# One-hot tables of a token's slot: two wide operations or one operation for each column, with the pieces of work around them moved

## The chip, the cores and the metric

The kernel runs on one core of a Trainium2 chip. A core has five engines, each with a queue of its own that it works through in order: TensorE (PE, matrix products, with PEld for the loading of its weights), VectorE (DVE), ScalarE (ACT), GpSimd (POOL) and SyncE (SP, which here only issues transfers). Engines wait for each other by semaphores. The metric is the time of one execution on the device in microseconds (us); lower is better. The kernel before takes 642.78 us, the median of three runs (641.9 to 643.16).

## What is computed

A layer normalisation of x (2 x 2048 tokens of 256 channels) feeds two branches, and both are added to x. One is a recurrent attention (RWKV), the other a mixture of eight experts of which each token uses two:

```python
k = (x * time_mix_k + last_x * (1.0 - time_mix_k)) @ Wk.T      # v, r in the same way
wkv = _wkv_scan(jnp.exp(k), v, td)      # den = den * td + kt ; num = num * td + kt * vt
out = jax.nn.sigmoid(r) * wkv @ Wo.T
...
scores = jax.nn.relu(jnp.einsum('bsd,de->bse', x, Wr) + br)
_, topk_idx = jax.lax.top_k(scores, K)
...
h = jax.nn.relu(jnp.einsum('bsd,edh->ebsh', x, W1) + b1[:, None, None, :])
y = jnp.einsum('ebsh,ehd->ebsd', h, W2) + b2[:, None, None, :]
out = jnp.einsum('bse,ebsd->bsd', router_weight, y)
```

The kernel does not compute all experts for all tokens. It sorts the tokens by expert and computes, for each expert, the tokens that chose it.

## The kernel before

The 4096 tokens are handled as 32 groups of 128 (NT = 32), and for the attention as 8 blocks of 512 tokens (NB = 8). There are four stretches of work.

**Front (0 to about 60 us).** The blocks are normalised, transposed and scored for the router. `table` in DRAM receives the normalised rows for later gathering.

**Routing (about 60 to 106 us).** Each of the 4096 x 2 choices gets a slot. There are NU = 74 units of 128 slots each. First the counts: two products (L650) give `pre`, whose half 1 (with `ones`) is the count of each expert in each group and whose half 0 (with `upper`) is the rank within the group. The scan L664 sums half 1. Some fifty tiny operations on VectorE follow, and at L773 to L778 each choice has its slot, cut into `lo` (its place in the unit, 0 to 127) and `hi` (its unit, 0 to 73). Then the map is inverted: for each slot, which token? This is a product of one-hot tables. For each of the 64 columns (2 choices x 32 groups) a table of `lo` (128 x 128) is the weights, and a table of `hi` times the token's number (128 x 74) is the moving operand; the 64 products are summed in `inv` (L873). VectorE builds the tables in eight chunks of CH = 8 columns: `oh_a` from `lo`, `oh_b` from `hi` (both by comparison with a ramp, L854), and `oh_t` = `oh_b` x `token` (L865). The tables are f16 with columns laid in pairs, so that each of the three operations covers the whole chunk at once. From `inv` come `into` (the row that a slot's result goes to) and `frm` (the row that it is gathered from), L879 to L886. `experts_of_places` (L790) finds which expert owns each unit; one product, `whose`, spreads it over the partitions, and `whose_i` holds it as an integer. SP reads `whose_i` and loads that expert's weights.

**Experts (about 113 to 607 us).** 32 steps of two or three units. A step gathers its tokens from `table` (POOL, L987, by `frm`), scales them (`unnorm`, L997), transposes them (`xp`, L1021), multiplies by the expert's `w1` (`hp`, L1032) and `w2` (`yp`, L1045), and adds the result to DRAM. The first step can start when `whose_i` has let SP load its weights and `frm` has let POOL gather its rows. VectorE does the attention's scans between.

**End (607 to 642 us).** The attention's last product (`op`, L1125) is added to what the experts left in DRAM and stored, block by block.

The order on every engine is written out by hand: the program's order is each queue's order. Two generators are used to fill gaps. `mix(n)` (L416) emits n blends of the attention's inputs on VectorE: two operations of 128 x 512 each, from a part that ScalarE has prepared ahead (`preparer`, L383). `some(n)` (L448) emits n pieces of the attention's projections on TensorE: four products of 128 x 512 (named `p`, L437), with ScalarE's eviction behind them. A block takes six pieces: two with `wk`, two with `wv`, two with `wr`, and each pair needs its own mix. In the table loop, `MIX` and `SOME` (L848) say after which chunk's tables a mix is put, and after which chunk's products a piece. The pieces are thus TensorE's work while VectorE builds tables, and there is a mix to be made for every two pieces. Blocks 5, 6 and 7 are mixed and projected around the tables; the last four pieces stand around L1067 to L1070, ahead of and behind `turn(0)`, which transposes the first step's tokens.

Of the kernel before, what the change touches and what calls it, by code (L numbers as in the profile page):

```python
# [26 lines left out]
def rwkv_moe_block(  # L27
# [21 lines left out]
    nc = tc.nc  # L49
    P = 128  # L50
    B, T, C = x.shape
    E, _, H = w1.shape
    K = 2
# [5 lines left out]
    NB = NTOK // TB  # L59
    BPS = T // TB  # L60
    NT = NTOK // P
# [13 lines left out]
    NU = U0 + 2 * NPAIR + NRARE  # L75
# [38 lines left out]
    rout = routing.enter_context(tc.tile_pool(name="rout", bufs=1))  # L114
# [76 lines left out]
    )  # L191
    CH = 8

    def ramp(nm, n):
        t = rout.tile([P, n, 2], F16, name=nm)
        nc.gpsimd.iota(
            t, [[1, n], [0, 2]], base=0, channel_multiplier=0,
            allow_small_or_imprecise_dtypes=True,
        )
        return t  # L200

    lo_iota, hi_iota = ramp("lo_iota", P), ramp("hi_iota", NU)
    at_pair = rout.tile([P, 1], F32, name="at_pair")
    at_unit = place[:, 1:2]
    wlim = rout.tile([P, 2 * E], F32, name="wlim")
# [11 lines left out]
    ones = const.tile([P, P], BF16, name="ones")  # L217
# [198 lines left out]
    def mix(n):  # L416
        for _ in range(n):
            next(blending)
# [29 lines left out]
    def some(n):  # L448
        for _ in range(n):
            next(projected)  # L450


    def rt(nm, shape=(P, NT, E), dtype=F32, tag=None):
        return rout.tile(list(shape), dtype, tag=tag or nm, name=nm)
# [59 lines left out]
    def vec(i, c):  # L514
# [14 lines left out]
    upper = const.tile([P, P], BF16, name="upper")  # L529
# [3 lines left out]
        pattern=[[1, P]], channel_multiplier=-1,  # L533
    )

    token = rout.tile([P, NT], F16, name="token")
    for i in range(2):
        nc.gpsimd.iota(
            token[:, i * HT : (i + 1) * HT], [[P, HT]], base=(-NTOK // 2, 1)[i],
            channel_multiplier=1, allow_small_or_imprecise_dtypes=True,  # L540
# [4 lines left out]
    for n, size in ((NTRI, 3), (NPAIR, 2), (NRARE, 1)):  # L545
# [3 lines left out]
            base=NTOK, channel_multiplier=1, allow_small_or_imprecise_dtypes=True,  # L549
# [96 lines left out]

    pre = ps_t.tile([P, 2, E * NT], F32, tag="pt", name="pre")
    hot_e = hot.rearrange("p t e -> p e t")
    for i, m in enumerate((upper, ones)):
        nc.tensor.matmul(  # L650
            pre[:, i, :].rearrange("p (e t) -> p e t", e=E), m, hot_e, start=True, stop=True
        )
# [121 lines left out]
    half = rt("half", (P, 2, K * NT), I32)  # L774
    nc.vector.tensor_scalar(half[:, 0, :], posi, P - 1, None, ALU.bitwise_and)
    nc.vector.tensor_scalar(half[:, 1, :], posi, 7, None, ALU.logical_shift_right)
    lohi = rt("lohi", (P, 2, K * NT), F16)
    nc.vector.tensor_copy(lohi, half)  # L778
    lo, hi = lohi[:, 0, :], lohi[:, 1, :]
    mix(0)  # L780
    some(2)


    whose_i = const.tile([P, NW], I32, name="whose_i")
# [3 lines left out]
    whose = ps_t.tile([P, NW], F32, tag="pt", name="whose")  # L788

    def experts_of_places():  # L790

        nc.vector.tensor_scalar(
            at_pair, place[:, 0:1], 0.5, NPAIR / 2, ALU.mult, ALU.add
        )
        nc.vector.tensor_copy(offs[:, 1:2], full)
        nc.vector.tensor_tensor(at_pair, at_pair, place[:, 0:1], ALU.min)
        lim = rt("lim", (P, 2, E))
        nc.vector.tensor_tensor(
            lim, fcum[:, 0:2, :], offs.unsqueeze(2).to_broadcast([P, 2, E]), ALU.add
        )  # L800
# [12 lines left out]
        nc.vector.tensor_scalar(  # L813
            held[:, 2, 0:E], fcum[:, 3, :], place[:, 0:1], None, ALU.is_le
        )
        by = rt("by", (P, 3))
        nc.vector.tensor_reduce(by, held, AX.X, ALU.add)
        paired = rt("paired", (P, 1))
        nc.vector.tensor_scalar(paired, nth, 0.0, None, ALU.is_lt)
        expert = rt("expert", (P, 1))  # L820
        nc.vector.tensor_scalar(
            expert, by[:, 0:1], by[:, 1:2], paired, ALU.subtract, ALU.mult
        )
        nc.vector.tensor_scalar(expert, expert, by[:, 1:2], float(E - 1), ALU.add, ALU.min)
        on_row = rt("on_row", (P, NW), BF16)
        nc.vector.tensor_scalar(
            on_row[:, W3:NW], ident[:, 0:NTRI], by[:, 2:3], float(E - 1), ALU.mult, ALU.min
        )
        nc.vector.tensor_scalar(on_row[:, 0:W3], ident[:, 0:W3], expert, None, ALU.mult)
        nc.tensor.matmul(whose, ones, on_row, start=True, stop=True)  # L830
        nc.vector.tensor_copy(whose_i, whose)

    def experts_later():
        last = rt("last", (P, 2))
# [10 lines left out]

    inv = ps_y.tile([P, NU], F32, tag="py", name="inv")
    opool = routing.enter_context(tc.tile_pool(name="opool", bufs=3))
    MIX, SOME = (0, 1, 0, 1, 0, 1, 0, 1), (1, 1, 1, 1, 1, 1, 1, 1)  # L848
    for i0 in range(0, K * NT, CH):

        tables = []
        for nm, n, src, ramp2 in (("a", P, lo, lo_iota), ("b", NU, hi, hi_iota)):
            t = opool.tile([P, CH // 2, n, 2], F16, tag=f"oh_{nm}", name=f"oh_{nm}_{i0}")
            nc.vector.tensor_tensor(  # L854
                t,
                ramp2.unsqueeze(1).to_broadcast([P, CH // 2, n, 2]),
                src[:, i0 : i0 + CH].rearrange("p (a b) -> p a b", b=2).unsqueeze(2)
                .to_broadcast([P, CH // 2, n, 2]),
                ALU.is_equal,
            )  # L860
            tables.append(t)
        a, bq = tables
        bt_ = opool.tile([P, CH // 2, NU, 2], F16, tag="oh_t", name=f"oh_t_{i0}")
        t0 = i0 % NT
        nc.vector.tensor_tensor(  # L865
            bt_, bq,
            token[:, t0 : t0 + CH].rearrange("p (a b) -> p a b", b=2).unsqueeze(2)
            .to_broadcast([P, CH // 2, NU, 2]),
            ALU.mult,
        )  # L870
        mix(MIX[i0 // CH])
        for i in range(CH):
            nc.tensor.matmul(  # L873
                inv, a[:, i // 2, :, i % 2], bt_[:, i // 2, :, i % 2],
                start=(i0 + i == 0), stop=(i0 + i == K * NT - 1),
            )
        some(SOME[i0 // CH])
    empty = rt("empty", (P, NU))
    nc.vector.scalar_tensor_tensor(empty, inv, 0.0, less, ALU.is_equal, ALU.mult)  # L879
    row = rt("row", (P, NU))  # L880
# [3 lines left out]
    nc.vector.scalar_tensor_tensor(into, row, float(NTOK // 2), empty, ALU.add, ALU.add)  # L884
    frm = const.tile([P, NU], I32, name="frm")
    nc.vector.tensor_scalar_min(frm, into, float(NTOK - 1))  # L886
    mix(1)
    some(2)
    experts_of_places()
    some(1)  # L890
    mix(1)
    some(2)
    mix(1)
    experts_later()
    routing.close()
# [68 lines left out]
    def load_first(s):  # L964
        ev = expert_of(s)
        pool = wpool if s % 3 else w1_own
        b1_sb = pool.tile([P, NH], F32, tag="b1", name=f"b1_{s}")
        nc.sync.dma_start(b1_sb, b1cols[bass.ds(ev, 1)].rearrange("a p h -> p (a h)"))
        w1_sb = pool.tile([P, NC, H], F32, tag="w1", name=f"w1_{s}")
        nc.sync.dma_start(w1_sb, w1[bass.ds(ev, 1)].rearrange("a (c p) h -> p (a c) h", p=P))  # L970
        weights[s, 1] = (w1_sb, b1_sb)
# [22 lines left out]
    def unnorm(s):  # L994

        for g in rows_of[s]:
            nc.vector.tensor_scalar(  # L997
                g[:, 0:C], g[:, 0:C], g[:, C + 3 : C + 4], None, ALU.mult
            )
# [64 lines left out]
    load_first(0)  # L1064
    load_second(0)
    load_first(1)
    some(1)  # L1067
    unnorm(0)
    turn(0)
    some(2)  # L1070
    gate(0)
    unnorm(1)
    gate(1)
# [4 lines left out]
    for s in range(NSTEP):  # L1078
# [8 lines left out]
        b, o = divmod(s, NC)  # L1087
# [26 lines left out]
    def as_rows(b, i):  # L1114
        return kvr[b][:, i].rearrange("p c t -> p (c t)").rearrange("p (n d) -> p n d", d=C)
# [4 lines left out]
    for i, (b, t) in enumerate(late):  # L1120
        pool, tag = pools[i // 2 % 4]
        op = pool.tile([P, 2, C], F32, tag=tag, name=f"op_{b}_{t}")
        for k in range(2):
            for c in range(NC):
                nc.tensor.matmul(  # L1125
                    op[:, k, :], kvr[b][:, 0, c, ts(t + k, P)], wo_sb[:, c, :],
                    start=(c == 0), stop=(c == NC - 1),
                )
        done = as_rows(b, 1)[:, t : t + 2, :]
        nc.vector.tensor_tensor(done, op, done, ALU.add)  # L1130
        if b == NB - 1:
            (nc.scalar, nc.sync)[i % 2].dma_start(out_l[b, :, t : t + 2, :], done)
        elif t:
            nc.scalar.dma_start(out_l[b], as_rows(b, 1))
# [61 lines left out]
```

## Time and profile before

One execution was profiled. Its own time was 643.74 us, of which the span of the instructions is 642.0.

| what | us |
|---|---|
| median of three runs | 642.78 |
| the profiled execution | 643.74 |
| its span | 642.0 |
| `hp` of the first step starts | 113.11 |
| the attention's last product starts | 607.68 |

Busy time by stretches of 20 us (a row is a stretch; the columns are the engines' busy us):

| stretch | PE | DVE | ACT | POOL | mean DMA GB/s |
|---|---|---|---|---|---|
| 60 to 80 | 19.99 | 16.82 | 13.38 | 0.88 | 162 |
| 80 to 100 | 18.30 | 19.54 | 10.75 | 0.71 | 0 |
| 100 to 120 | 20.00 | 12.65 | 8.82 | 10.17 | 254 |
| 120 to 140 | 20.00 | 13.26 | 6.34 | 6.32 | 228 |

The table stage is the row from 80 to 100. The clock granted to TensorE was full (1.00) in all four. Two instructions that overlap on one engine are counted once. In the timelines that follow, a line with xN stands for N like instructions in a row, from the first's start to the last's end; an instruction may start before the record of the one ahead of it on the engine ends, so the cost of one in a run is best read from start to start. A time in brackets is how long the engine stood idle before the row, and for whom.

### The profile page before, as it was taken

Reading aid. Unit: us, or ns where it says so; the run is one execution under the profiler, and the core shown is the slowest. Engines: PE = TensorE matmul, PEld = TensorE weight load, DVE = VectorE, ACT = ScalarE, POOL = GpSimd, SP = SyncE. Lnnn points to the kernel's source line nnn. Section 1 sums busy time; section 2 is a strip of 40 time slices with the busy share of each in tenths; the row PEclk is TensorE's granted clock in tenths of the full one; section 3 lists DMA queues with packets and bytes.
Section 4 is the critical chain, followed back from the end, with each engine's and each line's share of the span. In section 5 each row is a group of like instructions: output and inputs, shape, how many; then the busy total and the mean of one; then the engine's idle time right before and its main releaser. Section 6 shows DMA issues by size and latency. Waiting matters only on the chain.

```text
span 642.0 us, 8628 instructions
## 1 busy us (share of the span) xinstructions
PE 629.6 (98%) x2870; PEld 480.0 (75%) x2870; DVE 356.0 (55%) x814; ACT 207.7 (32%) x402; POOL 230.4 (36%) x201
## 2 busy tenths in 40 slices
PE   8999999999999999999999999999999999999995
PEld 3554444878687877878888888888888888888884
DVE  7996897767677684866888852222222222222132
ACT  5786654332322221322233332222222222222200
POOL 5780006035353352424344136334344433322200
PEclk9999999999999999999999999999999999999999
DMA  7835505857546364656556998765666666653177
GB/s 238 264 118 169 100 0 138 291 173 189 173 108 203 92 207 125 176 169 181 173 176 184 354 264 272 216 178 173 180 181 191 211 204 213 200 157 92 24 259 276
DMA packets 83944, 117.04 MB, mean 182 GB/s; under 512 B 14796, under 2 KB 70168, under 8 KB 83768
## 3 DMA queue, kind: packets, MB, share of 16 engines
q1 hardware_dynamic: 69196, 94.01, 44.7%
q0 software_dynamic: 13248, 18.24, 14.3%
q10 hardware_dynamic: 1452, 4.20, 1.7%
q8 instruction: 25, 0.41, 0.2%
q14 instruction: 23, 0.19, 0.1%
HBM read 98.50 MB, written 26.31 MB: 194 GB/s over the span
## 4 chain that ended last, share of the span: by engine, by line
PE 94%; DVE 3%; ACT 1%; DMA 0%; issue 0%; POOL 0%; DVEq 0%; ACTq 0%
PE hp L1032 38%; PE yp L1045 37%; PE p L437 11%; PE op L1125 4%; PE xp L1021 2%; PE tp L314 1%; PE p L352 1%; PE inv L873 0%; DMA x<-in_L_attn_x_dram 0%; DVE mix L407 0%; POOL rr_all L255 0%; ACT xaT L327 0%; ACT x2T L317 0%; PE pre L650 0%; PE sp L363 0%
## 5 line engine op out<-in xcount | busy, mean ns | idle before, releaser
L1032 PE MATMUL hp<-xT,w 128*128 128x256 f32 (+1 forms) x1024 | 246.5, 398 | 0.1
L1045 PE MATMUL yp<-w,h 128*128 128x256 f32 x1104 | 243.6, 379 | 0.0
L1036 ACT ACTIVATE h<-hp,b 128x256 f32<-128x256 f32 (+1 forms) x256 | 125.5, 490 | 352.2 <-PE hp L1032 217.5
L1045 PEld LDWEIGHTS yp<-w,h 128*128 128x128 f32 x1104 | 207.3, 190 | 26.9
L1032 PEld LDWEIGHTS hp<-xT,w 128*128 128x128 f32 x1024 | 181.5, 189 | 59.2 <-ACT h L1036 13.4
L1056 POOL DMA_INDIRECT out_dram<-y,into x36 | 58.8, 1634 | 157.0 <-DVE y L1050 107.4
L1056 POOL DMA_INDIRECT acc<-y,into x33 | 54.1, 1640 | 138.8 <-DVE y L1050 114.2
L987 POOL DMA_INDIRECT xg<-table,frm x69 | 81.6, 1183 | 50.6 <-PE p L437 29.8
L1022 DVE COPY xT<-xp 128x512 f32<-128x512 f32 (+1 forms) x37 | 23.8, 653 | 131.3 <-PE xp L1021 131.3
L1049 DVE TENSOR_TENSOR y<-yp,b 128x256 f32<-128x256 f32 x69 | 29.0, 421 | 112.4 <-PE yp L1045 107.1
L928 DVE RECIPROCAL dn<-dn 128x512 f32<-128x512 f32 x16 | 53.6, 3353 | 0.6
L440 ACT ACTIVATE kvr<-p 128x512 f32<-128x512 f32 x48 | 28.7, 599 | 33.8 <-PE p L437 32.4
L437 PE MATMUL p<-mix,wk 128*128 128x512 f32 x64 | 29.4, 599 | 0.8 <-DVE mix L323 0.8
L437 PE MATMUL p<-mix,wv 128*128 128x512 f32 x64 | 29.5, 597 | 0.0
L437 PE MATMUL p<-mix,wr 128*128 128x512 f32 x64 | 29.3, 596 | 0.1
L1125 PE MATMUL op<-wo,kvr 128*128 128x256 f32 x128 | 27.8, 379 | 0.0
L1050 DVE TENSOR_SCALAR y<-y,gate 128x256 f32<-128x256 f32 x69 | 26.3, 382 | 2.4
L1125 PEld LDWEIGHTS op<-wo,kvr 128*128 128x128 f32 x128 | 24.3, 190 | 3.3
L407 DVE SCALAR_TENSOR_TENSOR mix<-xaT,cols,mix 128x512 f32<-128x512 f32 x34 | 23.7, 743 | 2.2 <-ACT mix L372 2.2
L372 ACT ACTIVATE mix<-xaT,unmixed 128x512 f32<-128x512 f32 x34 | 24.1, 715 | 0.0
L437 PEld LDWEIGHTS p<-mix,wk 128*128 128x128 f32 x64 | 11.6, 190 | 13.9 <-issue 10.6
L997 DVE TENSOR_SCALAR xg<-xg 128x256 f32<-128x256 f32 x69 | 21.2, 351 | 0.0
(203 smaller groups left out, 382.9 us busy)
## 6 DMA issues: line engine op xcount, KB each, us to landing
w<-in_L_ffn_W_dram SPq DMA_DIRECT2D x64, 1024.0 KB, 9.0
table<-x SPq DMA_DIRECT2D x8, 512.0 KB, 3.4
b<-in_L_ffn_b_dram SPq DMA_DIRECT2D x32, 128.0 KB
kvr<-out_dram SPq DMA_DIRECT2D x16, 256.0 KB, 6.8
x<-in_L_attn_x_dram SPq DMA_DIRECT2D x7, 512.0 KB, 5.8
out_dram<-kvr ACTq DMA_DIRECT2D x7, 512.0 KB, 6.5
xg<-table,frm POOLq DMA_INDIRECT x69, 6.7
out_dram<-y,into POOLq DMA_INDIRECT x36, 5.5
```

Of the source, the lines that this page charges most:

```text
L372: nc.scalar.activation(m[:, c, :], xaTs[b][:, c, 0:TB], AF.Copy, scale=unmixed[:, i, c : c + 1])
L437: nc.tensor.matmul(p, w[:, c, ts(o, P)], m[:, c, :], start=(c == 0), stop=(c == NC - 1))
L440: nc.scalar.activation(kvr[b][:, i, o, :], p, f, scale=sign)
L928: nc.vector.reciprocal(dn, dn)
L987: nc.gpsimd.indirect_dma_start(out=g, out_offset=None, in_=table, in_offset=bass.IndirectOffsetOnAxis(ap=frm[:, u : u + 1], axis=0), bound ...
L1032: nc.tensor.matmul(hp, w1_sb[:, c, ts(j, P)], xT[:, c, :], start=(c == 0), stop=(c == NC - 1))
L1036: nc.scalar.activation(h[:, 0:n], hp, AF.Relu, bias=b1_sb[:, j : j + 1])
L1045: nc.tensor.matmul(yp, hs[j][:, ts(i, P)], w2_sb[:, j, :], start=(j == 0), stop=(j == NH - 1))
L1049: nc.vector.tensor_tensor(y, yp, b2_sb, ALU.add)
L1050: nc.vector.tensor_scalar(y, y, gates[s][i], None, ALU.mult)
L1056: return nc.gpsimd.indirect_dma_start(out=to, out_offset=bass.IndirectOffsetOnAxis(ap=into[:, u : u + 1], axis=0), in_=y, in_offset=None, ...
L1125: nc.tensor.matmul(op[:, k, :], kvr[b][:, 0, c, ts(t + k, P)], wo_sb[:, c, :], start=(c == 0), stop=(c == NC - 1),)
```

## The change

Seven things are changed; none alters what is computed.

1. `oh_b` and the wide `oh_t` are gone. `oh_t` is built by eight operations in each chunk, one for each column: a comparison of the ramp with the column's `hi` and a multiplication by its `token`, both given as one value per partition. `hi` and `token` are therefore f32, the ramp `hi_iota` is not doubled, and the table's columns lie one after the other. `oh_a` stays as it was.
2. `lo` and `hi` are made by two copies.
3. One mix and two more pieces stand in front of the table loop. In the loop, the last chunk has no mix and no piece behind it.
4. The product with `ones` comes before that with `upper`.
5. Behind the loop, a piece and `experts_of_places` come first, then a mix, then `whose_i`, and only then the five operations from `empty` to `frm`. The other mixes and pieces follow.
6. Around `turn(0)`, two pieces stand ahead of the transposes and one behind them, where it was one and two.
7. At the end, block 6 is stored in two halves (on ACT's and on SP's queue), as block 7 is.

```diff
-    def ramp(nm, n):
-        t = rout.tile([P, n, 2], F16, name=nm)
+    lo_iota = rout.tile([P, P, 2], F16, name="lo_iota")
+    hi_iota = rout.tile([P, NU], F16, name="hi_iota")
+    for t, pattern in ((lo_iota, [[1, P], [0, 2]]), (hi_iota, [[1, NU]])):
...
-    token = rout.tile([P, NT], F16, name="token")
+    token = rout.tile([P, NT], F32, name="token")
...
-    for i, m in enumerate((upper, ones)):
+    for i, m in ((1, ones), (0, upper)):
...
-    lohi = rt("lohi", (P, 2, K * NT), F16)
-    nc.vector.tensor_copy(lohi, half)
-    lo, hi = lohi[:, 0, :], lohi[:, 1, :]
-    mix(0)
-    some(2)
+    lo, hi = rt("lo", (P, K * NT), F16), rt("hi", (P, K * NT))
+    nc.vector.tensor_copy(lo, half[:, 0, :])
+    nc.vector.tensor_copy(hi, half[:, 1, :])
+    mix(1)
+    some(4)
...
-        nc.vector.tensor_copy(whose_i, whose)
...
-    MIX, SOME = (0, 1, 0, 1, 0, 1, 0, 1), (1, 1, 1, 1, 1, 1, 1, 1)
+    MIX, SOME = (0, 1, 0, 1, 0, 1, 0, 0), (1, 1, 1, 1, 1, 1, 1, 0)
     for i0 in range(0, K * NT, CH):
...
+        bt_ = opool.tile([P, CH, NU], F16, tag="oh_t", name=f"oh_t_{i0}")
+        for i in range(CH):
+            t = (i0 + i) % NT
+            nc.vector.tensor_scalar(
+                bt_[:, i, :], hi_iota, hi[:, i0 + i : i0 + i + 1], token[:, t : t + 1],
+                ALU.is_equal, ALU.mult,
             )
-            tables.append(t)
-        a, bq = tables
-        bt_ = opool.tile([P, CH // 2, NU, 2], F16, tag="oh_t", name=f"oh_t_{i0}")
-        t0 = i0 % NT
-        nc.vector.tensor_tensor(
-            bt_, bq,
-            token[:, t0 : t0 + CH].rearrange("p (a b) -> p a b", b=2).unsqueeze(2)
-            .to_broadcast([P, CH // 2, NU, 2]),
-            ALU.mult,
-        )
         mix(MIX[i0 // CH])
         for i in range(CH):
             nc.tensor.matmul(
-                inv, a[:, i // 2, :, i % 2], bt_[:, i // 2, :, i % 2],
+                inv, a[:, i // 2, :, i % 2], bt_[:, i, :],
                 start=(i0 + i == 0), stop=(i0 + i == K * NT - 1),
             )
         some(SOME[i0 // CH])
+    some(1)
+    experts_of_places()
+    mix(1)
+    nc.vector.tensor_copy(whose_i, whose)
     empty = rt("empty", (P, NU))
...
     nc.vector.tensor_scalar_min(frm, into, float(NTOK - 1))
+    some(2)
     mix(1)
-    some(2)
-    experts_of_places()
-    some(1)
-    mix(1)
-    some(2)
+    some(1)
     mix(1)
     experts_later()
...
-    some(1)
+    some(2)
     unnorm(0)
     turn(0)
-    some(2)
+    some(1)
...
-        if b == NB - 1:
+        if b >= NB - 2:
             (nc.scalar, nc.sync)[i % 2].dma_start(out_l[b, :, t : t + 2, :], done)
```

More of the change, by code (lines that the diff above doesn't have):

```diff
@@ L192, in rwkv_moe_block @@
     CH = 8
-    def ramp(nm, n):
-        t = rout.tile([P, n, 2], F16, name=nm)
+    lo_iota = rout.tile([P, P, 2], F16, name="lo_iota")
+    hi_iota = rout.tile([P, NU], F16, name="hi_iota")
+    for t, pattern in ((lo_iota, [[1, P], [0, 2]]), (hi_iota, [[1, NU]])):
         nc.gpsimd.iota(
-            t, [[1, n], [0, 2]], base=0, channel_multiplier=0,
-            allow_small_or_imprecise_dtypes=True,
-        )
-        return t
-    lo_iota, hi_iota = ramp("lo_iota", P), ramp("hi_iota", NU)
+            t, pattern, base=0, channel_multiplier=0, allow_small_or_imprecise_dtypes=True
+        )
     at_pair = rout.tile([P, 1], F32, name="at_pair")
@@ L847, in rwkv_moe_block @@
     opool = routing.enter_context(tc.tile_pool(name="opool", bufs=3))
-    MIX, SOME = (0, 1, 0, 1, 0, 1, 0, 1), (1, 1, 1, 1, 1, 1, 1, 1)
+    MIX, SOME = (0, 1, 0, 1, 0, 1, 0, 0), (1, 1, 1, 1, 1, 1, 1, 0)
     for i0 in range(0, K * NT, CH):
[L851 to L859, printed above, removed]
-            )
-            tables.append(t)
-        a, bq = tables
-        bt_ = opool.tile([P, CH // 2, NU, 2], F16, tag="oh_t", name=f"oh_t_{i0}")
-        t0 = i0 % NT
-        nc.vector.tensor_tensor(
-            bt_, bq,
-            token[:, t0 : t0 + CH].rearrange("p (a b) -> p a b", b=2).unsqueeze(2)
-            .to_broadcast([P, CH // 2, NU, 2]),
-            ALU.mult,
-        )
+        a = opool.tile([P, CH // 2, P, 2], F16, tag="oh_a", name=f"oh_a_{i0}")
+        nc.vector.tensor_tensor(
+            a,
+            lo_iota.unsqueeze(1).to_broadcast([P, CH // 2, P, 2]),
+            lo[:, i0 : i0 + CH].rearrange("p (a b) -> p a b", b=2).unsqueeze(2)
+            .to_broadcast([P, CH // 2, P, 2]),
+            ALU.is_equal,
+        )
+        bt_ = opool.tile([P, CH, NU], F16, tag="oh_t", name=f"oh_t_{i0}")
[4 more added lines that the diff above has]
+                ALU.is_equal, ALU.mult,
+            )
         mix(MIX[i0 // CH])
```

## The prediction

> **What bounds the kernel now.** I read the page first, for the engine with no idle time, then the timelines of TensorE and VectorE where the change sits (60 to 120 us), then the chain of waits through that stretch.
>
> ```profile
> PE 629.6 (98%) x2870; PEld 480.0 (75%) x2870; DVE 356.0 (55%) x814; ACT 207.7 (32%) x402; POOL 230.4 (36%) x201
> ```
>
> TensorE is the bound over the whole span: only 12.4 us of 642.0 are not counted busy. So the change can win little, and whatever makes TensorE wait adds in full: after 113 us the page's slices show it full, with nothing to absorb a delay. On average VectorE is half idle, but not in the table stage. TensorE there:
>
> ```profile
> 76.39 3.60 PE L437 MATMUL p<-mix,wk 128*128 128x512 f32 x8
> 81.70 0.45 PE L873 MATMUL inv<-oh_t,oh_a 128*128 128x74 f16 x8 [1.71 <-DVE oh_t L865]
> 81.99 1.96 PE L437 MATMUL p<-mix,wv 128*128 128x512 f32 x4
> 83.78 0.45 PE L873 MATMUL inv<-oh_t,oh_a 128*128 128x74 f16 x8
> 84.07 1.95 PE L437 MATMUL p<-mix,wv 128*128 128x512 f32 x4
> 85.98 0.45 PE L873 MATMUL inv<-oh_t,oh_a 128*128 128x74 f16 x8
> ```
>
> The columns are start, length, engine, line, operation; brackets hold the idle time ahead. One wait of 1.71 us precedes the first table, then chunks start 2.08 and 2.20 us apart. VectorE in the same place:
>
> ```profile
> 83.05 1.40 DVE L407 SCALAR_TENSOR_TENSOR mix<-xaT,cols,mix 128x512 f32<-128x512 f32 x2
> 84.37 0.68 DVE L854 TENSOR_TENSOR oh_a<-lo_iota,lohi 128x1024 f16<-128x1024 f16 x1
> 84.97 0.46 DVE L854 TENSOR_TENSOR oh_b<-hi_iota,lohi 128x592 f16<-128x592 f16 x1
> 85.46 0.47 DVE L865 TENSOR_TENSOR oh_t<-oh_b,token 128x592 f16<-128x592 f16 x1
> 85.85 0.69 DVE L854 TENSOR_TENSOR oh_a<-lo_iota,lohi 128x1024 f16<-128x1024 f16 x1
> ```
>
> No row carries idle time. From start to start: a mix costs 1.32, `oh_a` 0.60, `oh_b` 0.49, `oh_t` 0.39. A chunk is 1.48, two chunks and a mix 4.28: exactly TensorE's 2.08 + 2.20. The engines are level here, with VectorE ahead by a hair; TensorE's loss is 1.71 plus some 0.12 in every second chunk, about **2.1 us**. This is all that the change can win there.
>
> **Part 1: eight column operations for two wide ones.** Per chunk `oh_b` and `oh_t` go (0.88 us) and eight operations come, 128x74 f16 with two per-partition scalars (`hi`, `token`). None is in the trace, so I price one from these rows:
>
> ```profile
> 106.15 0.61 DVE L997 TENSOR_SCALAR xg<-xg 128x256 f32<-128x256 f32 x2
> ...
> 38.91 1.38 DVE L282 TENSOR_SCALAR x<-x,mv,rr_all 128x256 f32<-128x256 f32 x4
> 40.20 1.41 DVE L407 SCALAR_TENSOR_TENSOR mix<-dx,cols,xaT 128x512 f32<-128x512 f32 x2
> ```
>
> L997 has one such scalar: one takes 0.35, two together 0.61, so a further one costs 0.26. L282 has two: four take 1.29 to the next row's start, 0.32 each. 256 elements, one per cycle at 0.96 GHz (the Trainium skill, "VectorE: DVE Perf Modes", section "Specifications"), would stream in 0.267, more than L997's whole 0.26, so these run two per cycle (0.133); what remains is 0.13 fixed with one scalar and **0.187 with two**. A third row agrees: each half of the mix at L407 (one scalar, 512 elements, one per cycle, 0.533) follows the other in 0.66, again 0.13 fixed. Operations without such a scalar leave 0.07 (`oh_a`: 1024 at two per cycle is 0.533 of 0.60). Each scalar adds some 0.06.
>
> To 0.187 comes the stream of 74: 0.02 at four per cycle, 0.04 at two, 0.077 at one. The same page, section "The perf-mode tier table", gives a 16-bit one-source operation in SBUF four; no row here shows 16-bit ones. I take 0.02: **0.207 us per operation**, with 0.187 and 0.264 as the ends. Eight are 1.66 against 0.88; a chunk grows from 1.48 to 2.26.
>
> Here row and rule part. "Vector Engine (DVE) Microarchitecture Reference", section 5.2, gives a fixed cost of about 75 ns per instruction after overlap. That is the 0.07 of the rows without a scalar, but says nothing of the scalars. By it one operation would be 0.094 and a chunk 1.35, less than now: the change would pay. By L282 it doesn't. I follow the row, since it has the same two scalars. The first page's advice to minimise the count of operations (section "Rules for kernel authors") points the same way: 64 short ones replace 16 wide ones.
>
> **Part 2: order of the two `pre` products.** The scan L664 starts at 66.29, straight after the second product (65.62 + 0.63), and needs only `ones`, now first; VectorE itself is free at 65.67. The scan starts about 0.44 earlier, and so does the chain behind it, which shows no other wait. `upper` is read 1.3 us later; it isn't missed.
>
> **Part 3: a mix and two more pieces in front of the tables.** `mix(1)` puts 1.32 us on VectorE before the first table; `some(4)` gives TensorE 2 x 1.72 in its place (L437 pieces start 3.43 apart in twos). The inputs of both are ready: the piece uses a mix made at 74.9 to 77.5, and ScalarE's half of the new mix was computed by 76.3. Two smaller copies for one (`lo`, `hi`) cost 0.1. So VectorE: copies at 79.3, mix at 79.5, `oh_a` at 80.87, first table at 80.87 + 2.26 + 0.1 = 83.2. TensorE has work until 83.5. **The 1.71 us wait goes.**
>
> **Part 4: what is late next.** VectorE now needs 2 x 2.26 + 1.32 = 5.84 for two chunks, TensorE 4.2. The three mixes inside the loop follow chunks 1, 3 and 5, so the tables end at 80.87 + 8 x 2.26 + 3 x 1.32 = **102.9** instead of 95.9. TensorE, which would be through chunk 7 at 98.4, waits ahead of chunks 2, 4 and 6.
>
> Then the new tail. `experts_of_places` (99.60 to 102.1 in the trace, 2.5) comes before the next mix (1.4), and TensorE's next piece but one (`wk` of block 7) needs that mix: it starts at 102.9 + 2.5 + 1.4 = 106.8. Five pieces (8.6) lead to the transposes `xp` at 115.4, the transposes take 0.44, and one piece 1.72: `hp` starts at **117.5**, against 113.11: **+4.4**. As a formula, 104.3 + 64 times the price.
>
> **Part 5: gathers and weights.** `into` and `frm` move behind the experts, the mix and `whose_i`: `frm` is done at 107.95 instead of 98.36. POOL's first gather starts 0.93 later (99.29 now), the second 1.9 after that: 110.8. From `frm` to `xp` there were 10.9 us of cover (98.36 to 109.24), now 7.5. `whose_i` waits for TensorE's `whose` product, due at 105.6 behind `on_row` and so covered by the mix in front of it; were it late, `empty` to `frm` and every gather would queue behind it. It only moves from 102.7 to 106.9, so SP issues the first 1 MB `w1` at 108.2, ahead of the gathers; before, it went at 104.02, behind two gathers. Landing took 2.9 to 9.3 us in this stretch, median 6.2; the second gather, nearly alone, landed within 5.3 (101.18 to 106.5). With 5.5 and 0.4 for `unnorm` it is ready at 116.7: **1.3 us of wait** at `xp`, with 0 and 4 as the ends. `w1` has some 9 us until `hp`; it landed in about 5. Behind `unnorm(0)` on VectorE wait its gates and `unnorm(1)`, needed only after `hp`'s 7 us.
>
> **Part 6: the rest, at nothing.** The smaller iota and `token` in f32 lie at the start, on POOL. Block 6's store in two halves begins 0.7 us earlier, but the transfers are saturated there (384 to 427 GB/s from 632 to 636 us), and the last store still follows the last addition at 636.1: 0, with 0.3 either way.
>
> **Sum**: +4.4 + 1.3 = **+5.7** on the profiled execution's 643.74 (span 642.0), that is 649.4. It stands 1.0 above the median of the runs, so from 642.78 I say **648.5**.
>
> **Rivals.**
> *The column operations are cheap (faster).* At 0.094, VectorE's two chunks and a mix take 4.0, below TensorE's 4.2; both waits go, 2.1 us less: 640.7. It decides where the price falls below (113.1 - 104.3) / 64 = 0.138. For it: the 75 ns, and that no long run of this form is in the trace. Against it: three rows with scalars.
> *They stream one per cycle, or the gathers collide worse.* 0.264 each gives 121.2, +8.1, with 1.3 of wait +9.4: 652.2. A gather landing in 9.3 gives +4 on top of 4.4: 651.2. For it: the `w1` load now runs first. Against: gathers are only 130 KB.
> *A half price*, 0.15 to 0.18, as the scalar reads overlap in a run, and no wait at `xp`: +0.8 to +2.7, 643.6 to 645.5.
>
> **Chances.** Forecast's case (646 to 650.6) 0.62; dearer or collided 0.22; half price 0.08; cheap 0.08. The range of 8 in 10 leaves out the cheap case and the far ends: 645.0 to 652.5. Within 0.2% (1.3 us, about what a measurement of this kernel can tell from no change) takes a part of the half price: 0.03; faster 0.08; slower 0.89.
>
> **What would show it.** Right: columns at 0.2 us apart, chunk starts on TensorE alternately 2.3 and 3.6 apart, waits named `oh_t`, a wait at the `wk` piece for its mix, `frm` near 108, no wait before the first table. Wrong: columns near 0.1 apart and VectorE idle in the loop; or `hp` past 120 with `xp` waiting for its gather.

## The result and the profile after

The changed kernel takes **650.79 us** (median of four runs, 649.88 to 651.79) against 642.75 (four runs, 641.9 to 643.16): ratio 1.0125, 95% interval 1.011 to 1.0141. A second set of four runs of the same kernel, shown below, gave 649.37; all eight together have a median of 649.98. That is 7.1 us above 642.86, the median of the kernel before in the second set (35 runs). The profiled execution took 649.88, its span 648.2 against 642.0.

The page's line of busy times, for the kernel after:

```profile
PE 634.7 (98%) x2870; PEld 481.6 (74%) x2870; DVE 362.7 (56%) x863; ACT 207.7 (32%) x402; POOL 229.2 (35%) x201
```

Against the same line before, VectorE has 49 instructions more, 48 of them from 64 columns in place of 16 wide operations. TensorE has no instruction more, yet shows 5.1 us more as busy: products that follow each other slowly, because their tables come one column at a time, count as busy in a row. So the page's share hides most of the loss; the timeline shows it. Its columns are start, length, engine, line and operation, with the idle time ahead in brackets. First TensorE (L434 are the projection's pieces, L865 the tables' products):

```profile
80.06 3.60 PE L434 MATMUL p<-mix,wv 128*128 128x512 f32 x8
83.50 0.58 PE L865 MATMUL inv<-oh_t,oh_a 128*128 128x74 f16 x8
83.91 1.96 PE L434 MATMUL p<-mix,wr 128*128 128x512 f32 x4
85.70 0.65 PE L865 MATMUL inv<-oh_t,oh_a 128*128 128x74 f16 x8
86.19 1.96 PE L434 MATMUL p<-mix,wr 128*128 128x512 f32 x4
88.30 1.66 PE L865 MATMUL inv<-oh_t,oh_a 128*128 128x74 f16 x8
...
91.58 0.65 PE L865 MATMUL inv<-oh_t,oh_a 128*128 128x74 f16 x8
...
94.18 1.66 PE L865 MATMUL inv<-oh_t,oh_a 128*128 128x74 f16 x8 [0.15 <-DVE oh_t L859]
...
106.25 0.18 PE L827 MATMUL whose<-on_row,ones 128*128 128x37 bf16 x1 [0.47 <-DVE on_row L826]
107.00 3.67 PE L434 MATMUL p<-mix,wk 128*128 128x512 f32 x8 [0.57 <-DVE mix L404]
```

The wait ahead of the first table is gone. But from the third chunk on every second group of eight products takes 1.66 us instead of 0.45. Its products start 0.21 us apart, which is the pace of VectorE's columns below. The chunks start 2.6 and 3.3 us apart in turn. VectorE in the same place, without an idle moment:

```profile
80.13 1.41 DVE L404 SCALAR_TENSOR_TENSOR mix<-xaT,cols,mix 128x512 f32<-128x512 f32 x2
81.46 0.68 DVE L848 TENSOR_TENSOR oh_a<-lo_iota,lo 128x1024 f16<-128x1024 f16 x1
82.06 1.76 DVE L859 TENSOR_SCALAR oh_t<-hi_iota,hi,token 128x74 f16<-128x74 f16 x8
83.73 0.68 DVE L848 TENSOR_TENSOR oh_a<-lo_iota,lo 128x1024 f16<-128x1024 f16 x1
84.34 1.77 DVE L859 TENSOR_SCALAR oh_t<-hi_iota,hi,token 128x74 f16<-128x74 f16 x8
86.00 1.42 DVE L404 SCALAR_TENSOR_TENSOR mix<-xaT,cols,mix 128x512 f32<-128x512 f32 x2
```

Eight columns take 1.67 us from their start to the next row's (82.06 to 83.73), 0.209 each. Then the first step. First `hp` of the kernel before, in one row, then TensorE's rows and ScalarE's relus (L1029) of the kernel after:

```profile
113.11 7.07 PE L1032 MATMUL hp<-xT,w 128*128 128x256 f32 x32
...
115.66 0.38 PE L1014 MATMUL xp<-ident,xg 128*128 128x128 f32 x2
116.64 0.44 PE L1014 MATMUL xp<-ident,xg 128*128 128x128 f32 x2 [0.60 <-DVE xg L990]
...
118.64 4.62 PE L1025 MATMUL hp<-xT,w 128*128 128x256 f32 x20
124.24 2.86 PE L1025 MATMUL hp<-xT,w 128*128 128x256 f32 x12 [0.98 <-issue]
...
121.60 0.47 ACT L1029 ACTIVATE h<-hp,b 128x256 f32<-128x256 f32 x1 [0.56 <-PE hp L1025]
123.71 0.47 ACT L1029 ACTIVATE h<-hp,b 128x256 f32<-128x256 f32 x1 [1.64 <-issue]
124.50 0.47 ACT L1029 ACTIVATE h<-hp,b 128x256 f32<-128x256 f32 x1 [0.31 <-PE hp L1025]
```

`hp` of the first step starts at 118.64 instead of 113.11: **+5.53**. And it no longer runs through: now its products stop after 20, because ScalarE's fourth relu comes at 123.71, although the products that it reads (16 of the 20) end at about 122.3 in TensorE's records, some 1.4 us earlier. This gap is called the standstill below. TensorE is through with `hp` at 126.93, when the next transposes start, 8.29 us after its start instead of 6.91: **+1.38**. (Lengths of `hp` below are counted so, up to the transposes, where it has a gap; without one its row says 7.07.) The two make 6.91, and the attention's last product starts 6.92 later (614.43 against 607.51 in TensorE's rows, where the table ahead of the change has 607.68). Nothing is won or lost in the 490 us between. What follows that start is 0.7 us shorter in this execution, which makes +6.2 of the span.

### The profile page after: what moved, and what is told of

Read it like the earlier page. It is cut to its first block, busy times and chain, and to the rows that moved or that the text cites. A ratio compares the mean times of both kernels' runs of the same rounds, so it can differ in the third digit from the quotient of the medians.

```text
span 648.2 us, 8682 instructions
## 1 busy us (share of the span) xinstructions
PE 634.7 (98%) x2870; PEld 481.6 (74%) x2870; DVE 362.7 (56%) x863; ACT 207.7 (32%) x402; POOL 229.2 (35%) x201
## 4 chain that ended last, share of the span: by engine, by line
PE 89%; DVE 7%; DMA 1%; issue 1%; ACT 1%; POOL 0%; POOLq 0%; DVEq 0%; ACTq 0%
PE hp L1025 37%; PE yp L1038 37%; PE p L434 6%; PE op L1118 4%; PE xp L1014 2%; DVE oh_t L859 2%; DVE mix L404 1%; PE tp L311 1%; DVE oh_a L848 1%; DMA xg<-table,frm 1%; PE p L349 1%; DMA x<-in_L_attn_x_dram 0%; POOL rr_all L252 0%; ACT xaT L324 0%; ACT x2T L314 0%
## 5 line engine op out<-in xcount | busy, mean ns | idle before, releaser
L1029 ACT ACTIVATE h<-hp,b 128x256 f32<-128x256 f32 (+1 forms) x256 | 125.5, 490 | 353.6 <-PE hp L1025 215.5
L434 PE MATMUL p<-mix,wk 128*128 128x512 f32 x64 | 29.4, 599 | 1.4 <-DVE mix L320 0.8
L434 PE MATMUL p<-mix,wr 128*128 128x512 f32 x64 | 30.0, 600 | 0.0
L434 PE MATMUL p<-mix,wv 128*128 128x512 f32 x64 | 29.2, 595 | 0.0
L434 PEld LDWEIGHTS p<-mix,wk 128*128 128x128 f32 x64 | 11.6, 190 | 15.4 <-issue 10.3
```

Source lines behind the costliest of these rows:

```text
L434: nc.tensor.matmul(p, w[:, c, ts(o, P)], m[:, c, :], start=(c == 0), stop=(c == NC - 1))
L1029: nc.scalar.activation(h[:, 0:n], hp, AF.Relu, bias=b1_sb[:, j : j + 1])
```

## Experiments

### The changed kernel once more, and the two halves of the change alone

The first run is the changed kernel without any edit, for the spread of its time.

> The changed kernel once more, unaltered. Theory A expects 649.5 to 652, tables' end at 103.6, hp at 118.6 again. In the first profile the first step's eight hp columns took 1.4 us longer than 32 products take, with no releaser shown: if a refill of TensorE's instructions or a busy memory is the cause, it comes again in the same place and with a size that may differ; if it was a chance event, hp to the next xp takes 6.9 us.

Measured: 649.37 us (649.32 to 650.73), ratio 1.0106 (1.0088 to 1.0123). `hp` starts at 118.22 and takes 8.47 us; the late relus are now the third and the fourth. So the standstill in `hp` came in both profiles of this kernel, and its place and size vary a little.

The second run takes the columns out again (with `token` in f16 and `lo` and `hi` in one copy, as the wide form needs) and leaves everything else changed:

```diff
...
-        for i in range(CH):
-            t = (i0 + i) % NT
-            nc.vector.tensor_scalar(bt_[:, i, :], hi_iota, hi[...], token[...], ALU.is_equal, ALU.mult)
+        nc.vector.tensor_tensor(bt_, bq, token[...].to_broadcast([P, CH // 2, NU, 2]), ALU.mult)
...
```

> The changed kernel with the two wide operations per chunk put back (oh_b, oh_t, f16 token and halves); everything else as changed. Theory A (the price of the 64 column operations makes VectorE late): the tables end near 97.3 instead of 103.6, TensorE runs through the loop without waits, hp of the first step starts at 112 to 113.5 instead of 118.6, and the time is 641.5 to 644. Rival R (the moved order behind the loop, with frm late and the first weights ahead of the gathers, makes the loss): the time stays above 647, with a wait at xp of 3 us or more.

Measured: 643.56 us (642.89 to 644.87), ratio 1.0012 (1.0002 to 1.0022). `hp` starts at 112.13, 0.98 earlier than in the kernel before, but has a standstill too (8.06 us), so the last product starts 0.18 later than there (607.69). The third run is the opposite: the kernel before with the columns alone (`lo` and `hi` as two copies, `token` in f32), no mix or piece moved.

> The kernel before with the column operations alone; its order is kept. Theory A: the tables end near 102.1, the first table is late by 0.6 more than before, whose waits some 0.8 for VectorE, xp starts near 115.5 with its gather long landed, hp near 119.4: 648 to 650. Rival R: near the kernel before, under 645.

Measured: 649.27 us, ratio 1.0099 (1.0082 to 1.0116); `hp` starts at 119.64 and runs through in 7.07 us. So the columns alone cost 6.4 us (649.27 less 642.86, the kernel before in the same set), as much as they cost inside the whole change (649.98 less 643.56 is 6.4). All the rest of the change together is worth 0.7 us to the bad by the times (0.1 to 1.4 by the interval): it lets `hp` start 1.0 earlier (118.64 for 119.64 with the columns, 112.13 for 113.11 without), and the standstill takes that back.

### The front alone

That the rest does not pay is odd, since it removes the 1.71 us wait ahead of the first table. So the kernel before got only the mix and the two pieces in front, and the pieces that balance them:

```diff
-    mix(0)
-    some(2)
+    mix(1)
+    some(4)
...
-    MIX, SOME = (0, 1, 0, 1, 0, 1, 0, 1), (1, 1, 1, 1, 1, 1, 1, 1)
+    MIX, SOME = (0, 1, 0, 1, 0, 1, 0, 0), (1, 1, 1, 1, 1, 1, 1, 0)
...
-    some(2)
+    some(1)
```

> The kernel before with one mix and two pieces moved from the loop's end to its front; the wide tables and the order behind the loop are kept. Theory A (the front move is good by itself and was hidden by the columns): the 1.7 us wait before the first table goes, hp starts at 111 to 112, 640.5 to 642. Rival S (the mix in front only delays VectorE, and the wait comes back behind the loop): 642.5 to 644.

Measured: 643.46 us, ratio 1.0008 (1.0001 to 1.0015). The gain of 640.5 to 642 did not come; the time lies where the rival had it. The wait ahead of the first table is gone (its product starts at 83.36 without one). These are rows of VectorE, TensorE and ScalarE behind the loop in this run:

```profile
98.41 0.24 DVE L879 SCALAR_TENSOR_TENSOR empty<-inv,less 128x74 f32<-128x74 f32 x1 [1.15 <-PE inv L873]
...
100.37 1.96 PE L437 MATMUL p<-mix,wk 128*128 128x512 f32 x4 [0.20 <-DVE mix L407]
103.47 0.18 PE L830 MATMUL whose<-on_row,ones 128*128 128x37 bf16 x1 [1.14 <-DVE on_row L829]
...
112.60 1.89 PE L1032 MATMUL hp<-xT,w 128*128 128x256 f32 x8
115.77 5.45 PE L1032 MATMUL hp<-xT,w 128*128 128x256 f32 x24 [1.28 <-ACT h L1036]
...
115.24 0.84 ACT L1036 ACTIVATE h<-hp,b 128x256 f32<-128x256 f32 x2 [1.85 <-DVE kv L911]
```

The wait comes back behind the loop. The mix that now stands in front no longer stands behind the last chunk, and without it VectorE waits 1.15 us there for TensorE's last table. All that follows on VectorE comes 1.2 later, and TensorE in turn waits 0.20 us for a mix and 1.14 for `on_row`, the last step of `experts_of_places`, where the kernel before has no wait. Of the 1.71 us, 0.51 is left when `hp` starts (112.60 against 113.11).

Then `hp` stands still, here from the first relu on, and takes 8.45 us up to the next transposes in place of 6.91; the last product starts 1.04 later than in the kernel before (608.55). The view names `kv`, on which this relu doesn't depend: in the kernel before the first relu ran at 114.18, ahead of `kv` (114.46). The expert's bias `b`, which the relu also reads, was not late. SP issued it at 104.65, the 128 packets of 32 bytes (one for each partition) moved from 105.90 to 106.26, and ScalarE's wait for it is over at 112.84. What held the relu is not shown.

### The price of a column operation

The changed kernel with five groups of eight operations whose results nobody uses, put ahead of the tables: the column form with none, one and two per-partition scalars (the others constants), and the 256-element form with two and with none.

> The changed kernel with forty operations more on VectorE in front of the tables, for their price alone: eight each of 128x74 f16 with no per-partition scalar, with one, with two, then 128x256 f16 with two and with none. Theory A (each per-partition scalar adds a fixed 0.06 us, the stream runs four per cycle): 0.09, 0.15, 0.21, 0.25, 0.14 us from start to start. Rival (the cost is the instruction's, not the scalars'): the first three within 0.02 of each other. If the stream runs two per cycle, 128x256 with two scalars takes 0.32. The time is some 6 us above the changed kernel's and says nothing.

VectorE's rows of this run:

```profile
81.37 0.80 DVE L783 TENSOR_SCALAR trial<-hi_iota 128x74 f16<-128x74 f16 x8
82.08 1.28 DVE L785 TENSOR_SCALAR trial<-hi_iota,hi 128x74 f16<-128x74 f16 x8
83.27 1.76 DVE L789 TENSOR_SCALAR trial<-hi_iota,hi,token 128x74 f16<-128x74 f16 x8
84.95 2.13 DVE L794 TENSOR_SCALAR wide<-lo_iota,hi,token 128x256 f16<-128x256 f16 x8
87.00 1.16 DVE L799 TENSOR_SCALAR wide<-lo_iota 128x256 f16<-128x256 f16 x8
```

From row to row, divided by eight: 0.089 with no scalar, 0.149 with one, 0.210 with two, 0.256 for 256 elements with two, 0.135 with none. Each scalar costs 0.06; 182 more elements cost 0.046, which is near four elements a cycle at the 0.96 GHz that the prediction used (0.047). The form without scalars gives the same 0.046 for the same elements.

The time was not as expected: 663.26 us in the one execution, some 13 more than the changed kernel instead of 6.7 us of VectorE work. Most of the difference lies behind the tables, where the transposes wait 4.74 and 1.19 us for gathered rows. Ahead of them TensorE waited 5.46 us for the first table, and the windows view shows what came of that (columns: stretch and length, TensorE's busy time and instructions, granted clock, DMA share, GB/s):

```profile
78.00:83.00 5.00, 5.00 (x13) 1.00 0.00 0
83.00:88.00 5.00, 0.57 (x2) 0.84 0.00 0
88.00:90.00 2.00, 0.97 (x5) 0.50 0.03 8
90.00:92.00 2.00, 2.00 (x6) 0.50 0.01 4
92.00:94.00 2.00, 2.00 (x12) 0.69 0.00 0
94.00:96.00 2.00, 2.00 (x14) 1.00 0.00 0
```

The granted clock falls to half and stays there for over 4 us of work; it falls again (to a mean of 0.83) between 120 and 140, where the transposes wait. The Trainium skill, "TensorE: Matmul & The Clock Gate", section "What's actually happening", has an idle window of some 3.4 us halve this clock, and a busy one restore it, which this run fits. The run with the columns alone shows a half clock too, behind a wait of only 1.17 us, less than such a window, after which its first table's products crept along behind the columns:

```profile
81.26 1.57 PE L866 MATMUL inv<-oh_t,oh_a 128*128 128x74 f16 x8 [1.17 <-DVE oh_t L860]
82.67 2.71 PE L434 MATMUL p<-mix,wv 128*128 128x512 f32 x4
...
84.00:86.00 2.00, 2.00 (x11) 0.50 0.00 0
```

In the changed kernel, with more pieces in front, the clock stays at 1.00 throughout the tables.

### The scan that does not start earlier

The prediction let the scan start once the product with `ones` is done. It starts at 66.53, behind the second product as before. Here the product with `upper` was moved behind one more piece of the projection:

```diff
+    counted(1, ones)
...
-    some(4)
+    some(1)
+    counted(0, upper)
+    some(3)
```

> The changed kernel with the product with upper put behind one more piece, 1.7 us after that with ones. If the scan L664 waits only for ones, it starts about 0.45 us after ones begins plus its length, near 66.1, and the later addition to the rank waits for upper. If the scan waits for the whole of pre (both halves are one tile in one bank), it starts only after upper, near 68.2, and the tables come 1.7 us later. The changed kernel's trace (scan at 66.53, upper's end at 66.49) speaks for the second.

```profile
65.26 0.61 PE L647 MATMUL pre<-hot,ones 128*128 128x256 bf16 x1
67.43 0.61 PE L647 MATMUL pre<-hot,upper 128*128 128x256 bf16 x1
68.08 0.69 DVE L665 TENSOR_TENSOR_SCAN cum<-restart,pre 128x256 f32<-128x256 f32 x1 [2.34 <-PE pre L647]
```

The half that the scan reads is there at 65.87, and the scan starts at 68.08, right behind the other half (67.43 + 0.61). It waits for the last product that writes the tile `pre`, whichever half that is; item 4 of the change can therefore save nothing. The time was 649.8 us (one execution). `hp` starts some 1.6 us later than in the changed kernel (first relu at 121.26 for 119.70) and has no standstill.

### The standstill in the first `hp`

In the program relus two to eight wait for TensorE alone; no transfer, no other engine. One suspect is ScalarE's own supply of instructions. The Trainium skill, "Runtime: NRT & Kernel Launch", section "Instruction fetch mechanics", has each engine refill its instructions in blocks and calls the cost of crossing into the next "mostly hidden". If the fourth relu is where a block ends, instructions put ahead of it move that point. So the changed kernel got twelve tiny ScalarE copies, six before and six after the slots are computed, where ScalarE has time:

```diff
...
+    for i in range(6):
+        nc.scalar.copy(spare[:, i : i + 1], den_eps)
...
+    for i in range(6, 12):
+        nc.scalar.copy(spare[:, i : i + 1], den_eps)
```

> The changed kernel with twelve tiny copies more on ScalarE (six at 66 us, six in front of the tables), which only move its later instructions further along in its instruction stream. ScalarE stood still for 1.0 to 1.6 us in the first step's relu in the changed kernel, its repetition and the wide variant, with no releaser. Theory I (ScalarE waits there for a block of its own instructions): the stall moves twelve instructions ahead, onto the pieces' evictions, which have 1.1 us of slack each; hp of the first step takes 6.9 us and the time falls by 1 to 1.4. Theory M (a busy memory holds the relus up): the stall stays where it was and the time is that of the changed kernel, within 0.5.

The row of `hp` in this run:

```profile
118.53 7.07 PE L1030 MATMUL hp<-xT,w 128*128 128x256 f32 x32
```

It starts where it did and runs through; the relus follow each other 0.86 apart. 646.99 us (646.5 to 647.89), ratio 1.0069 (1.0054 to 1.0083): twelve instructions more and 3.0 us less than the 649.98 of the changed kernel. The standstill in the two profiles was 1.4 and 1.6 us, so something else must have shrunk. The control has the same twelve copies behind the first step's relus:

> The changed kernel with the same twelve tiny ScalarE copies as in the run before, but placed behind the relus of the first step instead of ahead of them. Theory (ScalarE's own stream of instructions reaches the end of a block in the middle of the first hp product, and only instructions ahead of that point move it): the standstill stays, hp(0) takes 8.2 to 8.5 us from first to last, and the time is 649 to 651. Rival (the twelve copies did something else, so that their place does not matter): hp(0) takes 7.07 us and the time is about 647.

Measured: 648.43 us (647.95 to 649.08), ratio 1.0086 (1.007 to 1.0101); `hp` starts at 118.39 and takes 7.99 us, with the fourth and the fifth relu late. So the standstill stays when the copies come late, but the time lies below the range given.

TensorE's rows show why. From the end of `hp` to the attention's last product it is 487.50 us in the changed kernel (126.93 to 614.43), 486.39 with the copies early (125.44 to 611.83) and 486.38 with them late (126.38 to 612.76). The copies save 1.1 us in later steps wherever they stand (four steps are 0.26 to 0.29 shorter), and their early place saves 1.2 to 1.4 more by the times. Why the later steps shorten was not asked.

Then the early copies in the version with wide tables, which also has a standstill (its `hp` starts at 112.13 and takes 8.06 us):

> The changed kernel with the wide tables put back, and the twelve tiny ScalarE copies early. Theory: hp(0) of this version took 8.06 us without the copies for the same standstill, so with them it takes 7.07 and the time falls from 643.6 to 641.8 to 642.8, with hp still beginning near 112.1. Rival (the standstill there has another cause, the late weights or the gathers): 643.5 as without the copies.

```profile
112.11 3.62 PE L1037 MATMUL hp<-xT,w 128*128 128x256 f32 x16
116.11 1.13 PE L1037 MATMUL hp<-xT,w 128*128 128x256 f32 x4 [0.38 <-issue]
118.24 2.86 PE L1037 MATMUL hp<-xT,w 128*128 128x256 f32 x12 [1.01 <-ACT h L1041]
...
115.58 0.47 ACT L1041 ACTIVATE h<-hp,b 128x256 f32<-128x256 f32 x1 [1.07 <-PE hp L1037]
117.72 0.84 ACT L1041 ACTIVATE h<-hp,b 128x256 f32<-128x256 f32 x2 [1.67 <-PE hp L1037]
```

The time fell as the theory had it, to 642.61 us (641.57 to 643.85), ratio 0.9994 (0.9987 to 1.0001), but not for its reason. In the profiled execution (643.45) the standstill is larger, `hp` takes 8.8 us, and the later steps are again 1.1 us shorter (486.38 for 487.50). Was the clean run chance? The same kernel again:

> The changed kernel with the twelve tiny ScalarE copies early, the same kernel as in the run that showed no standstill, once more, because the wide version with the same copies still showed one. If the copies take the standstill away each time: hp(0) takes 7.07 us without a gap, relus 0.86 apart, and the time is 646.5 to 647.9 again. Rival (the standstill comes and goes from one execution to the next, and its absence there was chance): hp(0) takes 8 us or more, with a late relu among the third to the fifth, and the time is 648 to 650.

Measured: 647.28 us (646.89 to 648.25), ratio 1.0069 (1.0052 to 1.0086), and again `hp` in one row of 7.07 us. So twice out of two the early copies took the standstill out of the changed kernel.

That an end of a block alone decides is refuted: the kernel before, the changed kernel and its version with wide tables all have the same 156 ScalarE instructions ahead of the first relu in the trace, and so has the run with `upper` moved; the first and the last show no standstill. Nor does the changed kernel's trace show a transfer of instructions while the fourth relu is late: two (8 and 16 KB) run from 119.85 to 121.30, none from 121.5 to 124.3, and the first run with early copies, which has no standstill, has two in the same place (120.25 to 121.30).

It is not even shown that ScalarE had its input. In the rows above, the view says that the late relus waited for TensorE's `hp`, though by TensorE's records the 16 products up to the fourth relu's end at 115.73. Such ends are modelled, so the products or their signals may have been late. The mark `issue` in the changed kernel says no more, since its first relus, which were on time, carry it too. The standstill is in seven of the fourteen profiles, that of the front alone included. Its cause stays open.

### Block 6 stored whole

```diff
-        if b >= NB - 2:
+        if b == NB - 1:
```

> The changed kernel with block 6 stored whole, as before the change, and all else as changed. The prediction's step (splitting the store of block 6 is worth 0 with 0.3 to either side): the time stays within 0.3 us of the changed kernel's 649.4 to 650.8. Rival (the shorter end seen after the change, 5.25 us behind the last addition against 5.97 before, is what the split brought): the time rises by 0.5 to 0.8 us and the end is again near 6.0 us.

Measured: 650.17 us (648.34 to 650.52), ratio 1.0102 (1.0086 to 1.0118), 0.2 from the 649.98 of the changed kernel: the split is worth nothing that can be seen, as predicted. From the start of the last product to the end of the span it is 34.5 us here and 33.7 in the changed kernel, but the first run with early copies and its repeat, both with the split, have 33.6 and 34.6. The stretch behind the last addition is 5.9 us again, as the rival had it, but it is 6.1 in that repeat too.

### A version that beats both

If the columns lose, and the gain in front comes back as a wait for `experts_of_places`, then the wide tables should stay and that work should leave VectorE. This kernel is the one before with the mix and the pieces in front, `experts_of_places` on GpSimd, nearly idle there (0.88 us busy from 60 to 80 before), a few of its operations rewritten for that engine, and `whose_i` in the middle of the table loop:

```diff
+    experts_of_places()            # its operations now nc.gpsimd
     MIX, SOME = (0, 1, 0, 1, 0, 1, 0, 1), (1, 1, 1, 1, 1, 1, 1, 0)
...
+        if i0 == CH:
+            told()                 # the product `whose`
...
+        if i0 == 3 * CH:
+            nc.vector.tensor_copy(whose_i, whose)
...
-    experts_of_places()
```

> A version to beat both: the kernel before with its wide tables, a mix and two pieces in front of the tables, and experts_of_places on GpSimd, idle until then, so that whose is multiplied behind the second chunk and whose_i is ready some 12 us earlier. VectorE has 2.5 us less to do behind the tables. If VectorE's tail and the late bias are what ate the gain of the front move, the whole 2.1 us comes out: no wait before the first table, none at whose, hp at 110.7 to 111.5, 640 to 641.3. If something else limits the first step (the gathers, ScalarE's standstill), 642 to 643.5.

Three rows of it, TensorE's `whose`, SP's issue of the bias (the first of the expert's weights) and TensorE's `hp`:

```profile
85.51 0.18 PE L837 MATMUL whose<-on_row,ones 128*128 128x37 bf16 x1
...
90.76 0.37 SPq L976 DMA_DIRECT2D b<-b1cols  x1
...
111.38 7.07 PE L1040 MATMUL hp<-xT,w 128*128 128x256 f32 x32
```

`whose` has no wait, the weights are issued 12.7 us earlier than in the kernel before, `hp` starts 1.73 earlier and runs through, and the last product also starts 1.73 earlier (605.78). **640.62 us** (639.52 to 642.09, nine runs) against 642.96: ratio 0.9967 (0.9956 to 0.9978), faster than the kernel before by 2.3 us and than the changed one by 9.4. The bias, part of what this run expected to win, was not late before; the wait for `on_row` was what could be won. Which of the moves let `hp` run through is not separated.

## Why the prediction was right, and where it was not

It said 648.5 us and slower; 650.79 was measured, within the range. The cause is the one it gave: by the runs with and without them, the columns alone cost 6.4 us.

**Part 1, the price.** Right: 0.209 in the changed kernel for 0.207, and 0.210 when measured by itself, with 0.06 for each scalar and four elements a cycle, as the rows had been read. The 75 ns of the Trainium skill ("Vector Engine (DVE) Microarchitecture Reference", section 5.2) would have said that the change pays; it is near the 0.089 of the form without scalars, and the two scalars are what it leaves out. The form with two scalars is far from the 0.138 at which the prediction's sum turns.

**Part 2, the scan 0.44 earlier.** Wrong. The half in the tile was ready; the wait is for the tile's last writer (66.53 in the changed kernel, for 66.29 before).

**Part 3, the wait goes.** Right: the first table's product starts at 83.50, just as TensorE's pieces end. But this is not a gain that lasts, as the 640.7 of the rival with cheap columns assumed: with the wide tables and the front alone, 1.34 of the 1.71 us came back as waits behind the loop, and the time was 643.46.

**Part 4, what is late next.** Right in mechanism and nearly in size: the tables end at 103.64 for 102.9 (0.44 of it the scan that gained nothing), `wk`'s piece waits for its mix and starts at 107.00 for 106.8, and two chunks take 5.88 for 5.84. On TensorE the two chunks split 2.6 and 3.3, not 2.3 and 3.6, since products start on single columns (0.21 apart in the slow groups).

**Part 5, gathers and weights.** The wait at `xp` exists, 0.60 for 1.3; the second gather was issued at 111.50 and had landed by 116.1, 4.6 us instead of 5.5. The transposes now fall into two halves, which costs 0.2. `hp` thus starts at 118.64, where +5.7 says 118.8. That it is so near is partly luck: the transposes were reached 0.3 late and cost 0.2 more, and the gather's wait was 0.7 shorter than forecast.

**What was missing from the sum** is the 1.38 us inside the first `hp`: the prediction took its 7 us as given. It makes +6.9 of +5.5, and +6.9 is what the last product's start shows, and near the eight runs' +7.1. Why it arises is open, as above. The other 0.9 of the first four runs' +8.0 lies within the spread of executions (649.88 to 651.79 for them, 649.32 to 650.73 for the second four).

**The rivals.** The cheap columns fall with the price. Dearer columns or colliding gathers would give 651 to 652.2, close to the time of the first set, but for reasons that the trace denies: the price is right and the gather landed early.

## What to carry to other kernels

Price a short VectorE operation by its per-partition scalars first and by its elements last: here 0.09, 0.15 and 0.21 us for none, one and two, while 74 elements stream in 0.02, so a wide operation with broadcast operands beat eight short ones that do two steps at once. Before counting a removed wait as a gain, look at the place that the work which fills it came from: here the mix was missed behind the loop, where 1.34 of the 1.71 us came back as waits, and a version that kept a mix there and moved 2.5 us of VectorE's work to a nearly idle engine kept the gain. And do not let an engine's busy share stand for its progress: TensorE's stayed at 98% while its products waited for one column at a time.

## What the runs showed of the hardware

- A tile written by two products is awaited as a whole: a reader of one half waited 2.2 us (65.87 to 68.08) for the other.
- How long the 4 KB bias takes to land depends on what was issued ahead of it. In the kernel before, the first was issued at 103.45 and its last signal came at 105.62, 2.2 us later; the next step's, issued at 107.73 behind 1 MB loads, took 10.5.
- TensorE's granted clock halved after a wait of 5.46 us and, in the run with the columns alone, after 1.17 us of idling with slow products behind it; a piece of four products then took 2.7 to 3.3 us in place of 1.96.
- In the first step, relus come up to 2 us after the recorded end of the products that they read, in seven of fourteen profiles, among them kernels that differ little from clean ones. Twelve tiny ScalarE copies ahead of them removed this in two of two profiles of one kernel and not in the profile of another.
- Twelve tiny ScalarE copies, early or late, shorten the steps behind the first by 1.1 us together (486.4 for 487.5), in all four profiles that have them.
